# Graph attention on one core: edge features and gathered rows in one tile, one 128-column product in the aggregation

## The chip, the cores and the metric

The kernel runs on one core of a Trainium2 chip. The metric is the device time of one execution in microseconds; three executions of the kernel before took 5133.07, 5138.95 and 5140.92 us, so the median is 5138.95 us. A core has TensorE (PE in the profile, with its weight loads shown apart as PEld), VectorE (DVE), ScalarE (ACT), GpSimd (POOL) and SyncE (SP), each with an instruction stream of its own that it works off in order, and 16 DMA engines that several queues feed.

## What is computed

A graph attention layer with a residual and a layer norm, over 12,500 nodes with 64 features and 400,000 edges with 64 features. The edges come sorted by their destination node `dst`; `src` is random.

```python
h_src = nfeats[src]
h_dst = nfeats[dst]
z_att = jnp.concatenate([h_src, h_dst, efeats], axis=-1)
e = jax.nn.leaky_relu(z_att @ W_attn + b_attn, negative_slope=0.01)[:, 0]
m = jnp.concatenate([h_src, efeats], axis=-1) @ W_ne
emax = jax.ops.segment_max(e, dst, num_segments=N)
ex = jnp.exp(e - emax[dst])
denom = jax.ops.segment_sum(ex, dst, num_segments=N)
alpha = ex / denom[dst]
z = jax.ops.segment_sum(alpha[:, None] * m, dst, num_segments=N)
out = jax.nn.relu(jnp.concatenate([nfeats, z], axis=-1) @ W_out)
return _layernorm(nfeats + out)
```

The kernel sums `alpha * [efeats, h_src]` by destination first (128 numbers per node, in the on-chip tensor `acc`, nodes along its columns) and multiplies by `W_ne` and `W_out` at the end.

## The kernel before

**Tiling.** Edges are worked on in groups of 512 (`GE`): 128 partitions (`P`) with `T` = 4 edges each. There are 782 groups. `SG` = 4 groups make a part, and `BG` = 32 groups, eight parts, a chunk. The 26 chunks have 30, 23 times 32, 12 and 4 groups. Since the edges are sorted, the edges of a group belong to few neighbouring nodes: a window of `S` = 48 nodes that starts at the group's first destination.

**Gather (L134 to L150).** For each part SP starts one DMA (L140) that loads the edges' features into a tile `ze` of [128, 4 groups, 4, 64] floats; a partition's four edges lie side by side in memory, so a group gives each partition a piece of 1 KB. POOL then issues 16 indirect DMAs (L149), one for each group and `t`, that fetch for each partition one row of a table in memory (64 node features and the source's attention term, 65 floats) into a second tile `zx` of [128, 4, 4, 65]. In the first chunk, where `plain` is true, the table doesn't exist yet; the rows come from `x`, and the source term is computed by DVE. Both tiles come from the pool `feats` with 11 buffers each (`ZB`): the eight parts of a chunk and three parts ahead. The gathers of a part can start when the part 11 earlier has been aggregated. `indices` (L112 to L118) turns the `src` numbers into the index tile `srcs`, two chunks ahead.

**Scores (L155 to L184).** SP loads a small row of window values (`wrow`, L159), PE spreads it over the partitions (`win`, L161), and DVE multiplies the edge features by their attention weights and sums them (L165, L167), adds the source term, which is column 64 of `zx` (L172), makes the one-hot mask `hot` of each edge's node in its window (L174), and takes the destination's term through the mask (L179, L182).

**Softmax (L224 to L319).** It runs once per chunk, for all eight parts: maxima and sums along sorted edges by scans on DVE, with small PE products (L190, L198, L247) between them. It ends in `alpha`, one weight per edge, and a factor `fac` that rescales what the last chunk left in a node that goes on.

**Aggregate (L321 to L342).** For each part DVE multiplies `hot` by `alpha` into `w` (L324, two buffers). PE then does, for each of the 16 pairs of group and `t`, two products into one PSUM tile `pg` (two buffers): stationary `ze` (64 columns) into partitions 0 to 63 and stationary `zx` (64 of its 65 columns) into partitions 64 to 127, each with the 48 columns of `w` moving, accumulated over `t` (L332). In float32 each is done in two passes, so it shows as two weight loads and two products. DVE adds each group's 48 columns to `acc` at the window's place (L342).

**Order.** `main` (L460 to L487) walks over the chunks: for each part of the chunk its tiles and scores, then the indices of the chunk two ahead, the softmax, and the aggregations. The order on each engine comes from a scheduler at build time, so on DVE and PE the aggregations of a chunk stand between the scores of the next one. From the third chunk on, 25 aggregations are each followed by `own_part`, which computes a piece of the nodes' own part of the result (L441 to L450). After the last chunk `finish_sorted` multiplies `acc` by the weights (L538) and does the norm.

Of the kernel before, what the change touches and what calls it, by code (L numbers as in the profile page):

```python
# [27 lines left out]
SG = 4  # L28
HQ = 4
EW = 65  # L30
ZB = 11
HB = 9
NBC = 4
# [5 lines left out]
def sorted_path(ctx, tc, x, dst, idx, edge, w_ne, w_attn, b_attn, w_out, out, flag):  # L39
# [6 lines left out]
    nc = tc.nc  # L46
    N, D = x.shape
# [6 lines left out]
    RP = REST // T  # L54
# [24 lines left out]

    table = dram.tile([NB * P, EW], F32, name="table")  # L80
    early = dram.tile([NB * P, D], F32, name="early")
# [51 lines left out]

    def gather(g0, n, srcs, b0, plain):  # L134

        ze = feats.tile([P, SG, T, D], F32, name="ze")
        zx = feats.tile([P, SG, T, EW], F32, name="zx")
        whole = min(n, NG - 1 - g0)
        if whole:
            nc.sync.dma_start(out=ze[:, 0:whole].rearrange("p g t f -> p g (t f)"),  # L140
                              in_=edge[g0 * GE:(g0 + whole) * GE, :].rearrange("(g p t) f -> p g (t f)", g=whole, t=T))
        if whole < n:
            nc.vector.memset(ze[:, n - 1], 0.0)
            nc.sync.dma_start(out=ze[0:RP, n - 1],
                              in_=edge[E - REST:E, :].rearrange("(p t) f -> p t f", t=T))
        for g in range(n):
            for t in range(T):
                at = srcs[:, t, g0 + g - b0:g0 + g - b0 + 1]
                nc.gpsimd.indirect_dma_start(  # L149
                    out=zx[:, g, t, 0:D] if plain else zx[:, g, t, :], out_offset=None,  # L150
                    in_=x[:, :] if plain else table[:, :],
                    in_offset=bass.IndirectOffsetOnAxis(ap=at, axis=0))
        return ze, zx

    def scores(g0, n, ze, zx, drel, b0, y, plain):  # L155

        b = g0 - b0
        wrow = tiny.tile([1, SG, S], F32, name="wrow")
        nc.sync.dma_start(out=wrow[:, 0:n, :], in_=wins[g0:g0 + n, :].unsqueeze(0))  # L159
        win = psum.tile([P, SG, S], F32, name="win", bufs=1)  # L160
        nc.tensor.matmul(win[:, 0:n, :], ones_row, wrow[:, 0:n, :], start=True, stop=True)  # L161

        yb = y[:, :, b:b + n].rearrange("p t g -> p g t")
        prod = work.tile([P, SG, T, D], F32, name="prod", bufs=1)
        nc.vector.tensor_tensor(prod[:, 0:n], ze[:, 0:n],  # L165
                                w_edge.unsqueeze(1).to_broadcast([P, n, T, D]), op=OP.mult)
        nc.vector.tensor_reduce(yb, prod[:, 0:n], axis=AX.X, op=OP.add)  # L167
        if plain:
            nc.vector.tensor_tensor(prod[:, 0:n], zx[:, 0:n, :, 0:D],
                                    w_src.unsqueeze(1).to_broadcast([P, n, T, D]), op=OP.mult)  # L170
            nc.vector.tensor_reduce(zx[:, 0:n, :, D], prod[:, 0:n], axis=AX.X, op=OP.add)
# [12 lines left out]
        nc.vector.scalar_tensor_tensor(yb, sdst[:, 0:n], SLOPE, sdst[:, 0:n], op0=OP.mult, op1=OP.max)  # L184
        return hot
# [135 lines left out]
    def aggregate(g0, n, ze, zx, hot, alpha, b0, fac):  # L321
        b = g0 - b0
        w = work.tile([P, SG, T, S], F32, name="w")
        nc.vector.tensor_tensor(  # L324
            w[:, 0:n], hot[:, 0:n],
            alpha[:, :, b:b + n].rearrange("p t g -> p g t").unsqueeze(3).to_broadcast([P, n, T, S]),
            op=OP.mult)
        pg = psum.tile([P, SG, P], F32, name="pg")[:, :, 0:S]
        for g in range(n):
            for t in range(T):  # L330
                for at, z in ((0, ze), (D, zx)):
                    nc.tensor.matmul(pg[at:at + D, g, :], z[:, g, t, 0:D], w[:, g, t, :],  # L332
                                     start=(t == 0), stop=(t == T - 1))
# [16 lines left out]
    while left > 0:  # L350
# [12 lines left out]
                        in_=dst[(NW - 1) * P * GE:E].rearrange("(e o) -> e o", o=1)[0:E - (NW - 1) * P * GE:GE, :])  # L363
# [13 lines left out]
    with tc.tile_pool(name="pre", bufs=2) as pre:  # L377
        d0f = pre.tile([1, NG], F32, name="d0f", bufs=1)
        nc.vector.tensor_copy(d0f, d0i)
        for g0 in range(0, NG, 3 * P):  # L380
            n = min(3 * P, NG - g0)
# [3 lines left out]
        for c0 in range(0, NB, CB):  # L385
            c1 = min(c0 + CB, NB)
            f1 = min(c1, NFULL)
            n = c1 - c0
            xt = pre.tile([P, CB, EW], F32, name="xt", bufs=3)
            if c1 > NFULL:  # L390
                nc.vector.memset(xt[:, NFULL - c0:NB - c0, :], 0.0)
                nc.scalar.dma_start(out=xt[0:TAIL, NFULL - c0, 0:D], in_=x[NFULL * P:N, :])
            if f1 > c0:
                nc.scalar.dma_start(
                    out=xt[:, 0:f1 - c0, 0:D],
                    in_=x[c0 * P:f1 * P, :].rearrange("(b p) f -> p b f", p=P))
            for k, to in ((0, xt[:, 0:n, D]), (1, sd[:, c0:c1])):
                prod = pre.tile([P, CB, D], F32, name="prod")
# [5 lines left out]
                out=table[c0 * P:c1 * P, :].rearrange("(b p) f -> p b f", p=P),  # L404
                in_=xt[:, 0:n, :])
# [9 lines left out]
        while len(ahead) < 5 and (len(ahead) + 1) * SG <= sizes[0]:  # L415
            ahead.append(gather(len(ahead) * SG, SG, prepared[0][0], 0, True))
        over = sdflat[0:1]
        nc.sync.dma_start(out=shifted, in_=bass.AP(over.tensor, over.offset, [[1, NB * P], [1, S]]))
        for k in range(NW):
# [3 lines left out]
                out=wk, out_offset=None, in_=shifted[:, :],  # L423
# [32 lines left out]
    def prepare(k):  # L456
        srcs, pp = prepared.pop(k) if k in prepared else indices(starts[k], sizes[k])
        return srcs, slots_of(starts[k], sizes[k], pp)

    with loop:  # L460
        carry = None
        own = 0
        ready = {k: prepare(k) for k in range(2)}
        for k, G in enumerate(sizes):
            b0 = starts[k]
            srcs, drel = ready.pop(k)
            d3 = neighbours(b0, G)
            y = rows.tile([P, T, BG], F32, name="y", bufs=2)
            if G < BG:
                nc.vector.memset(y[:, :, G:BG], 0.0)  # L470
            parts = []
            for g0 in range(b0, b0 + G, SG):
                n = min(SG, b0 + G - g0)
                ze, zx = ahead.pop(0) if ahead else gather(g0, n, srcs, b0, k == 0)
                hot = scores(g0, n, ze, zx, drel, b0, y, k == 0)
                parts.append((g0, n, ze, zx, hot))
# [3 lines left out]
            for g0, n, ze, zx, hot in parts:  # L480
                aggregate(g0, n, ze, zx, hot, alpha, b0, fac if g0 == b0 else None)
# [524 lines left out]
```

## Time and profile before

The profiled execution took 5109.14 us; its span, from the first instruction to the last, is 5107.4 us. TensorE's granted clock was 0.547 of full speed as a mean, and 0.5 in most slices. PEclk in the profile is that clock.

| What | Value |
|---|---|
| median of the runs | 5138.95 us |
| profiled execution | 5109.14 us |
| its span | 5107.4 us |
| PE busy with products / loads, 14,238 of each | 1410.6 / 1105.0 us |
| of these the aggregation's (L332), 12,512 of each | 1595.7 / 1410.3 us by single instructions, which overlap |
| POOL busy, 3,142 instructions | 2964.9 us |
| DVE busy, 4,006 instructions | 1708.1 us |
| gathers from the table (L149) | 3,008, 944 ns each |
| DMA queue of POOL (q0) | 100,320 packets, 104.41 MB, 10.6% |
| DMA queue of SP (q1) | 147,464 packets, 116.22 MB, 8.0% |
| DMA queue of ACT (q10) | 67,280 packets, 16.45 MB, 1.6% |
| edge loads (`ze`) | 194 of 512 KB, three smaller ones |

Queue shares are the time of the packets as a share of 16 engines' time over the span. In the answers about single instructions a line gives start and duration in microseconds, engine, line and operation, the tiles written and read, and, in brackets, how long the engine was idle before and what ended that. "issue" is time in which the engine waited for nothing that the profile shows, and "remote" is a semaphore whose sender the profile can't tell. The table of stretches gives, for each stretch, its length, the busy time of each engine with the number of instructions that started, the clock, the share of the DMA engines and their GB/s.

### The profile page before, as it was taken

What the parts mean: (1) busy time and instruction counts of PE and PEld (TensorE: products, weight loads), DVE (VectorE), ACT (ScalarE), POOL (GpSimd) and SP (SyncE); (2) the same over time, 40 slices, a digit from 0 to 9 for tenths busy, and PEclk for the clock granted to TensorE, in tenths of its full rate; (3) what the DMA queues carried; (4) which work ended last, traced back from release to release, by engine and by line L of the source; (5) the groups of instructions that cost most, each with busy time, mean ns of one, the idle gap of its engine ahead of it and who ended that gap; (6) DMA issues with size and microseconds to landing.
All of it is one profiled execution on the core that took longest, in us unless ns stands there. A gap on an engine that the chain in (4) does not pass through costs nothing.

```text
span 5107.4 us, 39846 instructions
## 1 busy us (share of the span) xinstructions
PE 1410.6 (28%) x14238; PEld 1105.0 (22%) x14238; DVE 1708.1 (33%) x4006; ACT 109.6 (2%) x239; POOL 2964.9 (58%) x3142
## 2 busy tenths in 40 slices
PE   0022233443222222222222222222222222222226
PEld 0012122332222122212121212122222211221225
DVE  3333233232342332332323323323233233233346
ACT  0000000000000000000000000000000000000001
POOL 6645656556556556565565565655655655656550
PEclk9975555555555555555555555555555555555555
DMA  6111122222111112111111111111111211212113
GB/s 145 25 34 42 44 48 54 53 53 60 41 45 44 43 38 48 42 46 41 43 44 43 42 44 43 43 42 44 47 41 40 47 42 38 47 37 48 41 36 77
DMA packets 315273, 239.73 MB, mean 47 GB/s; under 512 B 160576, under 2 KB 264235, under 8 KB 315064
## 3 DMA queue, kind: packets, MB, share of 16 engines
q0 software_dynamic: 100320, 104.41, 10.6%
q1 hardware_dynamic: 147464, 116.22, 8.0%
q10 hardware_dynamic: 67280, 16.45, 1.6%
q8 instruction: 115, 1.88, 0.2%
q14 instruction: 94, 0.77, 0.1%
HBM read 226.98 MB, written 12.28 MB: 47 GB/s over the span
## 4 chain that ended last, share of the span: by engine, by line
issue 28%; POOL 26%; another core or an unknown queue 19%; DVE 14%; PE 10%; DMA 3%; DVEq 1%; ACT 0%; POOLq 0%; ACTq 0%
POOL zx L149 26%; PE pg L332 7%; DMA zx<-table,srcs 2%; DVE y L167 2%; DVE prod L165 2%; DVE sdst L182 1%; DVE prod L179 1%; PE sm L198 1%; PE sm L190 1%; DVE hot L174 1%; DVE w L324 1%; DVE by_row L195 0%; DVE b L271 0%; DVE acc L342 0%
## 5 line engine op out<-in xcount | busy, mean ns | idle before, releaser
L149 POOL DMA_INDIRECT zx<-table,srcs x3008 | 2840.6, 944 | 1951.4 <-issue 841.3
L332 PE MATMUL pg<-w,ze 128*64 128x48 f32 x6256 | 792.3, 297 | 1640.2 <-issue 985.1
L332 PEld LDWEIGHTS pg<-w,ze 128*64 128x64 f32 x6256 | 703.6, 213 | 1729.3 <-issue 1581.7
L332 PE MATMUL pg<-w,zx 128*64 128x48 f32 x6256 | 803.4, 297 | 613.2 <-issue 582.1
L324 DVE TENSOR_TENSOR w<-hot,alpha 128x768 f32<-128x768 bf16 x196 | 184.0, 949 | 2208.2 <-remote 1135.9
L332 PEld LDWEIGHTS pg<-w,zx 128*64 128x64 f32 x6256 | 706.7, 213 | 656.3 <-issue 621.7
L342 DVE TENSOR_TENSOR acc<-acc,pg 128x48 f32 x782 | 153.9, 197 | 812.7 <-remote 742.1
L161 PE MATMUL win<-wrow,ones_row 1*128 1x192 f32 (+1 forms) x392 | 182.0, 552 | 746.8 <-DVE prod L179 433.1
L161 PEld LDWEIGHTS win<-wrow,ones_row 1*128 1x128 f32 x392 | 92.9, 284 | 810.4 <-DVE prod L179 448.3
L165 DVE TENSOR_TENSOR prod<-ze,fixed 128x1024 f32<-128x1024 f32 x196 | 236.9, 1209 | 19.9 <-issue 19.9
L167 DVE TENSOR_REDUCE y<-prod 128x16 f32<-128x1024 f32 x196 | 236.1, 1205 | 2.4 <-DVE y L184 2.3
L182 DVE TENSOR_REDUCE sdst<-prod 128x16 f32<-128x768 f32 x196 | 185.1, 944 | 4.3 <-DVE prod L179 2.4
L179 DVE TENSOR_TENSOR prod<-hot,win 128x768 f32<-128x768 bf16 x196 | 185.4, 946 | 0.9 <-issue 0.2
L174 DVE TENSOR_TENSOR hot<-fixed,drel 128x768 bf16<-128x768 f32 x196 | 185.6, 947 | 0.0
L149 POOL DMA_INDIRECT zx<-in_x_dram,srcs x120 | 116.9, 974 | 51.5 <-issue 36.3
L112 ACT ACTIVATE nat<-raw 32x1024 f32<-32x1024 int32 (+3 forms) x26 | 27.5, 1056 | 3242.2 <-PE pp L115 1762.9
L450 PE MATMUL pg<-wout,xtt 64*128 64x64 f32 x196 | 47.4, 418 | 132.0 <-ACT xtt L447 132.0
L198 PE MATMUL sm<-ones_row,by_row 1*128 1x1 f32 x208 | 59.2, 351 | 81.2 <-DVE by_row L195 66.2
L198 PEld LDWEIGHTS sm<-ones_row,by_row 1*128 1x128 f32 x208 | 50.9, 302 | 131.5 <-DVE by_row L195 104.2
L190 PE MATMUL sm<-order,b 128*1 128x128 f32 x104 | 30.1, 391 | 163.8 <-DVE b L271 158.4
L450 PEld LDWEIGHTS pg<-wout,xtt 64*128 64x128 f32 x196 | 42.8, 319 | 148.3 <-ACT xtt L447 148.3
L190 PE MATMUL sm<-order,s 128*1 128x128 f32 x104 | 30.3, 393 | 147.7 <-issue 57.1
(133 smaller groups left out, 949.1 us busy)
## 6 DMA issues: line engine op xcount, KB each, us to landing
ze<-in_edge_dram SPq DMA_DIRECT2D x194, 512.0 KB
zx<-table,srcs POOLq DMA_INDIRECT x3008
table<-xt ACTq DMA_DIRECT2D x14, 227.5 KB
wrow<-wins SPq DMA_DIRECT2D x195, 0.8 KB
xb<-in_x_dram ACTq DMA_DIRECT2D x24, 128.0 KB
early<-xo ACTq DMA_DIRECT2D x24, 128.0 KB
xb<-in_x_dram ACTq DMA_DIRECT2D x12, 256.0 KB
xo<-early SPq DMA_DIRECT2D x12, 256.0 KB
```

The costliest lines, as they stand in the source:

```text
L149: nc.gpsimd.indirect_dma_start(out=zx[:, g, t, 0:D] if plain else zx[:, g, t, :], out_offset=None, in_=x[:, :] if plain else table[:, :], ...
L161: nc.tensor.matmul(win[:, 0:n, :], ones_row, wrow[:, 0:n, :], start=True, stop=True)
L165: nc.vector.tensor_tensor(prod[:, 0:n], ze[:, 0:n], w_edge.unsqueeze(1).to_broadcast([P, n, T, D]), op=OP.mult)
L167: nc.vector.tensor_reduce(yb, prod[:, 0:n], axis=AX.X, op=OP.add)
L174: nc.vector.tensor_tensor(hot[:, 0:n], slots.unsqueeze(1).unsqueeze(1).to_broadcast([P, n, T, S]), drel[:, :, b:b + n].rearrange("p t g -> ...
L179: nc.vector.tensor_tensor(at[:, 0:n], hot[:, 0:n], win[:, 0:n].unsqueeze(2).to_broadcast([P, n, T, S]), op=OP.mult)
L182: nc.vector.tensor_reduce(sdst[:, 0:n], at[:, 0:n], axis=AX.X, op=OP.add)
L190: nc.tensor.matmul(p[0:1, :], col, order, start=True, stop=True)
L198: nc.tensor.matmul(p[:, 0:1], by_row, ones_row[:, 0:1], start=True, stop=True)
L324: nc.vector.tensor_tensor(w[:, 0:n], hot[:, 0:n], alpha[:, :, b:b + n].rearrange("p t g -> p g t").unsqueeze(3).to_broadcast([P, n, T, S]) ...
L332: nc.tensor.matmul(pg[at:at + D, g, :], z[:, g, t, 0:D], w[:, g, t, :], start=(t == 0), stop=(t == T - 1))
L342: nc.vector.tensor_tensor(ag, ag, pg[:, g, :], op=OP.add)
```

## The change

The two tiles become one, `z`, of [128, 4, 4, 129] floats (`ZW` = 129), from the same pool with 11 buffers: columns 0 to 63 hold the edge's features, 64 to 127 the gathered node's, and column 128 its attention term. It takes as many bytes as the two did.

- The edge load becomes one DMA per group, 4 per part, of 128 KB each. A partition's four edges still lie side by side in memory (1 KB), but in the tile they stand 516 bytes apart, in pieces of 256 bytes.
- The gathers write into columns 64 to 128 of `z`; their number and size stay.
- The scores read the same numbers out of `z`, at its stride.
- The aggregation does one product per group and `t`, with the 128 columns of `z` as the stationary operand, into all 128 partitions of `pg`, where it did two with 64 columns each.

```diff
+ZW = 129
...
-        ze = feats.tile([P, SG, T, D], F32, name="ze")
-        zx = feats.tile([P, SG, T, EW], F32, name="zx")
+        z = feats.tile([P, SG, T, ZW], F32, name="z")
         whole = min(n, NG - 1 - g0)
-        if whole:
-            nc.sync.dma_start(out=ze[:, 0:whole].rearrange("p g t f -> p g (t f)"),
-                              in_=edge[g0 * GE:(g0 + whole) * GE, :].rearrange("(g p t) f -> p g (t f)", g=whole, t=T))
+        for g in range(whole):
+            nc.sync.dma_start(out=z[:, g, :, 0:D],
+                              in_=edge[(g0 + g) * GE:(g0 + g + 1) * GE, :].rearrange("(p t) f -> p t f", t=T))
...
                 nc.gpsimd.indirect_dma_start(
-                    out=zx[:, g, t, 0:D] if plain else zx[:, g, t, :], out_offset=None,
+                    out=z[:, g, t, D:2 * D] if plain else z[:, g, t, D:ZW], out_offset=None,
...
-        nc.vector.tensor_tensor(prod[:, 0:n], ze[:, 0:n],
+        nc.vector.tensor_tensor(prod[:, 0:n], z[:, 0:n, :, 0:D],
                                 w_edge.unsqueeze(1).to_broadcast([P, n, T, D]), op=OP.mult)
...
-        nc.vector.tensor_tensor(yb, yb, zx[:, 0:n, :, D], op=OP.add)
+        nc.vector.tensor_tensor(yb, yb, z[:, 0:n, :, 2 * D], op=OP.add)
...
         for g in range(n):
             for t in range(T):
-                for at, z in ((0, ze), (D, zx)):
-                    nc.tensor.matmul(pg[at:at + D, g, :], z[:, g, t, 0:D], w[:, g, t, :],
-                                     start=(t == 0), stop=(t == T - 1))
+                nc.tensor.matmul(pg[:, g, :], z[:, g, t, 0:2 * D], w[:, g, t, :],
+                                 start=(t == 0), stop=(t == T - 1))
```

More of the change, by code (lines that the diff above doesn't have):

```diff
@@ L134, in gather @@
     def gather(g0, n, srcs, b0, plain):
-        ze = feats.tile([P, SG, T, D], F32, name="ze")
-        zx = feats.tile([P, SG, T, EW], F32, name="zx")
+        z = feats.tile([P, SG, T, ZW], F32, name="z")
         whole = min(n, NG - 1 - g0)
-        if whole:
-            nc.sync.dma_start(out=ze[:, 0:whole].rearrange("p g t f -> p g (t f)"),
-                              in_=edge[g0 * GE:(g0 + whole) * GE, :].rearrange("(g p t) f -> p g (t f)", g=whole, t=T))
+        for g in range(whole):
+            nc.sync.dma_start(out=z[:, g, :, 0:D],
+                              in_=edge[(g0 + g) * GE:(g0 + g + 1) * GE, :].rearrange("(p t) f -> p t f", t=T))
         if whole < n:
-            nc.vector.memset(ze[:, n - 1], 0.0)
-            nc.sync.dma_start(out=ze[0:RP, n - 1],
+            nc.vector.memset(z[:, n - 1, :, 0:D], 0.0)
+            nc.sync.dma_start(out=z[0:RP, n - 1, :, 0:D],
                               in_=edge[E - REST:E, :].rearrange("(p t) f -> p t f", t=T))
@@ L149, in gather, with scores @@
                 nc.gpsimd.indirect_dma_start(
-                    out=zx[:, g, t, 0:D] if plain else zx[:, g, t, :], out_offset=None,
+                    out=z[:, g, t, D:2 * D] if plain else z[:, g, t, D:ZW], out_offset=None,
                     in_=x[:, :] if plain else table[:, :],
                     in_offset=bass.IndirectOffsetOnAxis(ap=at, axis=0))
-        return ze, zx
-    def scores(g0, n, ze, zx, drel, b0, y, plain):
+        return z
+    def scores(g0, n, z, drel, b0, y, plain):
         b = g0 - b0
@@ L168, in scores @@
         if plain:
-            nc.vector.tensor_tensor(prod[:, 0:n], zx[:, 0:n, :, 0:D],
+            nc.vector.tensor_tensor(prod[:, 0:n], z[:, 0:n, :, D:2 * D],
                                     w_src.unsqueeze(1).to_broadcast([P, n, T, D]), op=OP.mult)
-            nc.vector.tensor_reduce(zx[:, 0:n, :, D], prod[:, 0:n], axis=AX.X, op=OP.add)
-        nc.vector.tensor_tensor(yb, yb, zx[:, 0:n, :, D], op=OP.add)
+            nc.vector.tensor_reduce(z[:, 0:n, :, 2 * D], prod[:, 0:n], axis=AX.X, op=OP.add)
+        nc.vector.tensor_tensor(yb, yb, z[:, 0:n, :, 2 * D], op=OP.add)
         hot = work.tile([P, SG, T, S], BF16, name="hot", bufs=HB)
@@ L319, in softmax, with aggregate @@
         return alpha, fac, (top[:, R:R + 1], den[:, R:R + 1])
-    def aggregate(g0, n, ze, zx, hot, alpha, b0, fac):
+    def aggregate(g0, n, z, hot, alpha, b0, fac):
         b = g0 - b0
@@ L473, in sorted_path @@
                 n = min(SG, b0 + G - g0)
-                ze, zx = ahead.pop(0) if ahead else gather(g0, n, srcs, b0, k == 0)
-                hot = scores(g0, n, ze, zx, drel, b0, y, k == 0)
-                parts.append((g0, n, ze, zx, hot))
+                z = ahead.pop(0) if ahead else gather(g0, n, srcs, b0, k == 0)
+                hot = scores(g0, n, z, drel, b0, y, k == 0)
+                parts.append((g0, n, z, hot))
             if k + 2 < len(sizes):
@@ L479, in sorted_path @@
             alpha, fac, carry = softmax(G, y, d3, carry, k == 0)
-            for g0, n, ze, zx, hot in parts:
-                aggregate(g0, n, ze, zx, hot, alpha, b0, fac if g0 == b0 else None)
+            for g0, n, z, hot in parts:
+                aggregate(g0, n, z, hot, alpha, b0, fac if g0 == b0 else None)
                 if own < NB and k > 1:
```

## The prediction

> **What bounds the kernel now.** I read the page's busy shares first, then the chain of waits, then the gathers' line with what its idle time ended on, then one chunk of the middle along POOL and PE.
>
> ```profile
> PE 1410.6 (28%) x14238; PEld 1105.0 (22%) x14238; DVE 1708.1 (33%) x4006; ACT 109.6 (2%) x239; POOL 2964.9 (58%) x3142
> ...
> issue 28%; POOL 26%; another core or an unknown queue 19%; DVE 14%; PE 10%; DMA 3%; DVEq 1%; ACT 0%; POOLq 0%; ACTq 0%
> ```
>
> No engine is full; POOL is nearest. It only issues gathers, on a fixed beat:
>
> ```profile
> L149 POOL DMA_INDIRECT zx<-table,srcs x3008: 938/944/1131, 175.2 to 4969.6; - x188
> ...
>   PE pg L332: 786.6, 62
>   remote: 252.8, 80
> ```
>
> ```profile
> 2204.00 0.95 POOL L149 DMA_INDIRECT zx<-table,srcs  x1 [0.30 <-issue]
> 2211.60 0.94 POOL L149 DMA_INDIRECT zx<-table,srcs  x1 [6.64 <-PE pg L332]
> 2212.85 0.94 POOL L149 DMA_INDIRECT zx<-table,srcs  x1 [0.30 <-issue]
> ...
> 2320.82 0.94 POOL L149 DMA_INDIRECT zx<-table,srcs  x1 [20.97 <-PE pg L332]
> ```
>
> The beat is 0.944 + 0.30 = 1.247 us, so a part (16 gathers) takes 19.97 us, a chunk of eight parts 160, and all 3,128 gathers 3,901. The rest of the profiled 5,109 is about 150 us before the first and after the last gather, and 786.6 + 252.8 less 142 usual pauses of 0.30, 997 us, in which POOL waits for a slot that an aggregation by PE has to release. In the chunk shown (first gathers at 2118.7 and 2320.8, 202 us apart) the waits above 0.30 are 6.7, 6.3, 2.6, 3.0 and 2.9 us between aggregations, 21.5 together, and 20.7 while DVE finishes the softmax. The full chunks repeat this within about a microsecond.
>
> Why is PE, 28% busy, late? The table of stretches for the aggregation's line alone, for part 0 (no gathers in flight), a stretch with gathers, and the wait after it:
>
> ```profile
> core 0: us, PE busy (x) PEld busy (x), PEclk, DMA share, GB/s
> 2114.70:2118.50 3.80, 3.75 (x70) 3.75 (x72) 0.50 0.07 14
> ...
> 2138.40:2158.40 20.00, 1.91 (x8) 1.45 (x8) 0.50 0.14 27
> 2158.40:2165.30 6.90, 2.28 (x25) 1.89 (x24) 0.50 0.02 5
> ```
>
> The clock is 0.50 in all three, yet 70 products start in 3.8 us without gathers and 8 in 20 us with them. The timeline of PE shows the change of pace:
>
> ```profile
> 2136.71 0.31 PE L332 MATMUL pg<-w,ze 128*64 128x48 f32 x1
> 2139.19 0.24 PE L332 MATMUL pg<-w,zx 128*64 128x48 f32 x1 [2.17 <-issue]
> 2141.99 0.24 PE L332 MATMUL pg<-w,ze 128*64 128x48 f32 x1 [2.56 <-issue]
> ```
>
> Starts of loads and products in that stretch fall on a grid of 0.70 us (2137.80, 2139.19, 2140.59, 2141.99, 2142.70), about one record per one or two steps, until 4 us after the last gather was issued. What makes the grid the trace does not say.
>
> **The change, part by part.**
>
> *Half the PE instructions.* A part had 16 x 2 logical products of two passes, each a load and a product: 128 instructions; it will have 64. Part 2 of this chunk ran about 62 instructions at full pace from 2135.08, then some 26 to 38 grid steps to 2163.69, then the last 40 at full pace. If a step costs 0.70 us per instruction whatever its width, 64 instructions are the 62 fast ones and at most a few steps: done near 2143 instead of 2165. The lower bound is that nothing is saved: a load of 128 columns takes two steps where one of 64 took one, and 64 x 2 is again 128 steps. The rows lie nearer the first: the load (64 columns) and the product (48 rows) hold the same grid though they differ in size. I take the 21.5 us per chunk as gone, over 22 full chunks: -473 us; ends 0 and -542 (997 less 22 x 20.7).
>
> *One wide product for two narrow ones.* At full pace the two narrow tiles run side by side: part 0 of the next chunk starts at 2316.85 and is released at 2320.56, 3.7 us. The nearest row for a 128-column stationary is the final stage:
>
> ```profile
> 5039.63 17.33 PE L538 MATMUL po<-both,acc 128*128 128x64 f32 x80 [0.32 <-DVE both L520]
> ```
>
> 17.33 / 80 is 0.217 us per load and product with 64 moving rows; the load's share is about half (loads start 0.107 after a product), so 48 rows give 0.107 + 0.75 x 0.11 = 0.19, and 32 pairs 6.1 us: 2.4 us longer than today, with ends 0 (32 x 0.107 = 3.4, if load and product overlap) and +3.2 (0.217). It counts where POOL waits with no gathers in flight, at part 0 of each chunk after the first: 25 x 2.4 = +60 us (0 to +80). For the other parts it hides behind the 20 us of gathers; with that cover gone it is 2.4 us at each of 195 parts, +468.
>
> The Trainium skill speaks against this step: "TensorEngine Tiling (Array Packing)", sections Key Properties and Theoretical Speedup, says that different tiles load and multiply in parallel and that a dimension of 64 or less may gain up to 2x. By it undoing the split doubles 3.7 us to 7.4 and the +60 becomes 93. The trace agrees on the narrow side (ze and zx products start 0.01 us apart); the wide side no row of this kernel shows at 48.
>
> *Edge loads.* One DMA of 512 KB in 1-KB pieces becomes four of 128 KB in 256-B pieces. SP issues one in 0.37 to 0.39 us (2132.87), so 3 x 0.38 = 1.1 us more per part, ahead of the window row's load and the next loads in SP's queue; SP waits most of the time for releases, so 0 on the path. On the queues:
>
> ```profile
> q1 hardware_dynamic: 147464, 116.22, 8.0%
> q10 hardware_dynamic: 67280, 16.45, 1.6%
> ```
>
> Engine time per packet is 8.0% x 16 x 5107 / 147,464 = 44 ns on q1 and 19 ns on q10, whose packets are mostly 245 B. A part's edges take 512 x 44 / 16 = 1.4 us now and 2,048 x 19 / 16 = 2.4 us then, up to 5.6 at 44 ns: +1.0 to +4.2 us of transfer. It starts with the part's first gather and has the 20 us of the other gathers as cover, since the scores need both: 0. POOL kept its beat at 2133.68 while the edge load that SP issued at 2132.87 ran. Without that cover: +195 to +820.
>
> The skill's "DMA: Bandwidth & Descriptors", Why small descriptors are slow (HBM only), gives 27% overhead for 256-byte descriptors; by it alone 1.4 us would become 1.8. The rows above allow for more, and they decide.
>
> *Waits and DVE.* The new tile holds the 129 columns of the two old ones; gathers, sums and DVE's operations stay, and a wider stride changes no element count: 0. The first gather of a part gets waits on the old edge loads of its slot, which landed some 200 us before. A semaphore event on POOL takes 0.043 us and at 2223.995 it lay inside the 0.30 us pause: 0, at most 354 more of them x 0.043 = +15. SP's in-order queue sees the same release as today.
>
> **Sum.** 5109 - 473 + 60 = 4,696 in the profiled execution; the median of the runs is 5138.95 / 5109.14 = 1.0058 of it, so 4,723, say **4,720**. The softmax's wait of 20.7 us stays: after the last release DVE still has some 41 us of scores and softmax (2279.8 to 2320.5), of which a part of gathers covers 20.
>
> **Rivals.**
>
> *Slower: the grid stays and the wide product comes on top.* If steps go by columns, every release still waits for the gathers to stop, and then the burst that ends the part is serial. Price 2.4 us at the six of eight releases that POOL waits for, 146 in all, +351: 5,460, runs 5,490; at all 195 parts +468, runs 5,610. It decides if a 128-column load takes 1.4 us on the grid. For it: part 5's records end at 2218.7 and yet its release comes at 2233.9, 2.6 us after the last gather's issue, as if the end of the flow and not the count set it; chunks with additional PE work keep gaps of 3.4 us. Against: part 1 was released at 2132.9 in the midst of the flow.
>
> *The count does not matter and nothing else bites.* The gaps stay, part 0 pays 2.4: 5,169, runs 5,200, 1.2% slower; with overlap of load and product no change.
>
> *All waits go.* With releases early, DVE reaches the last scores as soon as they land, 100 us into a chunk of 160, and 41 us later the softmax is done: no wait at all. 5109 - 22 x 42.2 = 4,181, runs 4,205. Against: at 28 grid steps per 20 us of gathers PE can't do 64 instructions a part without some pause.
>
> **Chances.** Forecast 0.34 (its own range 4,480 to 4,930), all waits gone 0.16, count without effect 0.14, slower 0.36. Leaving out the outer ends of both: 4,250 to 5,550. A difference of about 0.2% is what a measurement here can tell from none. Faster 0.50 (the first two), same 0.04 (from the count without effect, with overlap), slower 0.46.
>
> **What would show it.** Right: POOL's idle time on PE's aggregation falls from 1,039 towards 550 us, a wait of some 23 us per chunk remains, q1 has about 450,000 packets, and aggregations end in mid-flow. Wrong: loads 1.4 us apart on the grid, or five gaps per chunk as before and each longer; gathers off their 1.247 beat while q1 runs; part 0 at 3.7 us or above 7.

## The result, and the profile after

The changed kernel took 5315.73 us (median of 4 runs, 5298.48 to 5325.86), the kernel before in the same comparison 5137.34 us: a ratio of 1.034, 95% interval 1.032 to 1.037. It is slower by 3.4%, where 4,720 us, 8% faster, was forecast. The profiled execution has a span of 5296.8 us, 189.4 us more than that of before.

The experiments showed that chips differ here. On some the kernel before takes 5,121 to 5,137 us, as in the first comparison; on others 4,104 to 4,111 us. The difference lies in how PE fares while gathers are in flight. I call them the slow and the quick kind; every ratio below is taken on one chip. The experiments ran on eight chips, four of each kind, each on one occasion only; that the chip itself makes the difference is likely but not shown. On the quick kind the variants with the wide product lose 1.1%; the changed kernel itself was not run there.

The page of the changed kernel, its busy shares, chain, gathers, products and two queues:

```profile
PE 1879.7 (35%) x7982; PEld 1675.6 (32%) x7982; DVE 1719.2 (32%) x4006; ACT 107.9 (2%) x239; POOL 2961.6 (56%) x3142
...
q0 software_dynamic: 100320, 104.41, 12.9%
q1 hardware_dynamic: 456824, 116.26, 10.2%
...
another core or an unknown queue 44%; issue 15%; POOL 13%; DVE 12%; PE 10%; DMA 2%; ACTq 2%; DVEq 1%; ACT 0%; POOLq 0%; SPq 0%
...
L331 PE MATMUL pg<-w,z 128*128 128x48 f32 x6256 | 1381.7, 409 | 1795.7 <-DVE acc L341 1072.5
```

The change does what it says: PE has 7,982 products where it had 14,238, and q1 moves the same bytes in 456,824 packets. But PE's busy time goes up, from 1410.6 to 1879.7 us: two narrow products ran side by side, and a wide one runs alone. What POOL waited for, from the gathers' line:

```profile
L149 POOL DMA_INDIRECT z<-table,srcs x3008: 938/944/1087, 174.9 to 5121.6; - x188
...
  PE pg L331: 861.2, 45
  remote: 295.0, 57
```

102 waits instead of 142, but 1,156 us instead of 1,039. The beat of the gathers has stayed at 944 ns. One chunk of the middle on POOL:

```profile
2122.88 0.94 POOL L149 DMA_INDIRECT z<-table,srcs  x1 [6.26 <-PE pg L331]
...
2161.57 0.95 POOL L149 DMA_INDIRECT z<-table,srcs  x1 [0.30 <-issue]
2194.12 0.95 POOL L149 DMA_INDIRECT z<-table,srcs  x1 [31.60 <-PE pg L331]
```

The pauses between aggregations now come once in two parts, about 6 us each, instead of five per chunk; that is where fewer instructions helped. The wait for the softmax has grown from 21 to 31 us. I summed all POOL waits above the usual 0.30 us from the starts of the gathers in the two traces (per chunk: means of chunks 7 to 23, which have no work of `own_part`):

| us | before | after | difference |
|---|---|---|---|
| waits for the softmax, all (per chunk) | 538.9 (20.9) | 751.6 (30.5) | +212.7 |
| waits between aggregations, all (per chunk) | 496.7 (21.7) | 443.5 (17.9) | -53.2 |
| from the last gather to the last aggregation | 64.9 | 101.3 | +36.4 |
| from there to the end | 72.0 | 73.0 | +1.0 |

The rows make +196.9, where the span grew by 189.4. The first gather starts 1.9 us earlier, the gathers' own time is 3.3 us less in all, and about 2 us are left over in small pauses.

### The profile page after: what moved, and what is told of

Its sections match the earlier page's. It is cut to its first block, busy times and chain, and to the rows that moved or that the text cites. A ratio compares the mean times of both kernels' runs of the same rounds, so it can differ in the third digit from the quotient of the medians.

```text
span 5296.8 us, 29642 instructions
## 1 busy us (share of the span) xinstructions
PE 1879.7 (35%) x7982; PEld 1675.6 (32%) x7982; DVE 1719.2 (32%) x4006; ACT 107.9 (2%) x239; POOL 2961.6 (56%) x3142
## 3 DMA queue, kind: packets, MB, share of 16 engines
q1 hardware_dynamic: 456824, 116.26, 10.2%
## 4 chain that ended last, share of the span: by engine, by line
another core or an unknown queue 44%; issue 15%; POOL 13%; DVE 12%; PE 10%; DMA 2%; ACTq 2%; DVEq 1%; ACT 0%; POOLq 0%; SPq 0%
POOL z L149 13%; PE pg L331 7%; DVE prod L165 2%; ACTq L113 1%; DVE y L167 1%; DVE sdst L182 1%; DMA z<-table,srcs 1%; PE sm L198 1%; PE sm L190 1%; DVE prod L179 1%; DVE hot L174 1%; PE win L161 1%; DVE acc L341 0%; DVE by_row L195 0%
## 5 line engine op out<-in xcount | busy, mean ns | idle before, releaser
L149 POOL DMA_INDIRECT z<-table,srcs x3008 | 2838.1, 944 | 2108.5 <-PE pg L331 861.2
L331 PE MATMUL pg<-w,z 128*128 128x48 f32 x6256 | 1381.7, 409 | 1795.7 <-DVE acc L341 1072.5
L331 PEld LDWEIGHTS pg<-w,z 128*128 128x128 f32 x6256 | 1361.1, 330 | 1869.7 <-DVE acc L341 1080.3
L161 PE MATMUL win<-wrow,ones_row 1*128 1x192 f32 (+1 forms) x392 | 196.0, 593 | 536.0 <-issue 379.7
L165 DVE TENSOR_TENSOR prod<-z,fixed 128x1024 f32<-128x1024 f32 x196 | 238.5, 1217 | 16.4 <-issue 16.0
L190 PE MATMUL sm<-order,s 128*1 128x128 f32 x104 | 30.5, 396 | 441.0 <-issue 310.4
L149 POOL DMA_INDIRECT z<-in_x_dram,srcs x120 | 116.1, 968 | 49.6 <-issue 36.0
L256 DVE TENSOR_TENSOR_SCAN s<-pf,e 128x128 f32<-128x128 f32 x26 | 11.0, 423 | 291.2 <-ACT e L254 235.3
L190 PE MATMUL sm<-order,b 128*1 128x128 f32 x104 | 30.5, 395 | 130.7 <-DVE b L271 99.7
```

The costliest lines, as they stand in the source:

```text
L149: nc.gpsimd.indirect_dma_start(out=z[:, g, t, D:2 * D] if plain else z[:, g, t, D:ZW], out_offset=None, in_=x[:, :] if plain else table[:, :],
L165: nc.vector.tensor_tensor(prod[:, 0:n], z[:, 0:n, :, 0:D], w_edge.unsqueeze(1).to_broadcast([P, n, T, D]), op=OP.mult)
L190: nc.tensor.matmul(p[0:1, :], col, order, start=True, stop=True)
L331: nc.tensor.matmul(pg[:, g, :], z[:, g, t, 0:2 * D], w[:, g, t, :], start=(t == 0), stop=(t == T - 1))
```

## Where the three differences come from

**The wide product itself.** The table of stretches for the aggregation's line, for part 0 after the softmax and for the time behind the last gather of the changed kernel, then for the latter in the one before. The columns are the stretch, its length, busy time and number of products, of loads, the clock, the share of the DMA engines and GB/s. The 1.00 of the first two lines is no measurement (see the last section):

```profile
2186.70:2194.10 7.40, 7.32 (x35) 7.32 (x35) 1.00 0.04 7
5122.50:5223.80 101.30, 62.67 (x288) 61.71 (x288) 1.00 0.01 1
```

```profile
4970.60:5035.40 64.80, 26.96 (x606) 25.85 (x607) 0.66 0.02 3
```

Part 0 starts at 2186.78 and POOL goes on at 2194.12, 7.3 us later, where it was 4.0 (2316.85 to 2320.82): 3.4 us at each chunk's softmax, over 80 us in all. Behind the last gather nine more parts (288 products of 32 a part) follow one after the other; PE is busy 62.7 us there instead of 27.0, and this +35.7 is the +36.4 of the table. The pace can be read off any of them:

```profile
5128.41 7.06 PE L331 MATMUL pg<-w,z 128*128 128x48 f32 x32 [10.81 <-DVE acc L341]
```

7.06 / 32 is 0.22 us per load and product, as in the final stage with 64 moving rows (0.217): the 16 rows less save nothing. Part of the +35.7 can be the clock's and not the width's: in that stretch of the kernel before it was 0.66 as a mean, and its pairs of narrow products start 0.107 us apart at 0.50 and 0.058 at 1.00, while the wide products at full pace are 0.21 us apart throughout. At 0.50 the 303 pairs would have taken 32 us instead of 27, an estimate from these numbers.

**The waits between aggregations.** Two of the five waits per chunk are gone, the others have changed. In the kernel before, 34 of the 85 waits over 0.5 us in chunks 7 to 23 end 0.3 us after the recorded end of the last product of the part that POOL waits for; they are the long ones, 6.4 us each (23 of 101 in a second trace). The other 51 are for parts recorded done 2 to 20 us before. In the changed kernel all 52 waits are of this second sort: the part is recorded done 12 to 32 us before POOL goes on. PE's timeline before the wait that ends at 2122.88, and DVE's first use of the sum:

```profile
2092.34 7.06 PE L331 MATMUL pg<-w,z 128*128 128x48 f32 x32 [5.40 <-issue]
...
2104.74 0.24 PE L331 MATMUL pg<-w,z 128*128 128x48 f32 x1 [2.32 <-issue]
2107.55 0.24 PE L331 MATMUL pg<-w,z 128*128 128x48 f32 x1 [2.57 <-issue]
...
2122.64 0.21 DVE L341 TENSOR_TENSOR acc<-acc,pg 128x48 f32 x1 [24.36 <-PE pg L331]
```

The 32 products of the part in question run at full pace with gathers in flight and are recorded done at 2099.40. The last gather of the flow ends at 2116.6, and only 6 us after that do DVE and POOL go on, 23 us after the part's end. The products of the next part stand on the steps of the kernel before: 1.40 us from a load (2103.34) to its product (2104.74), as with half the columns (1.39, 2137.80 to 2139.19). So a wide instruction costs no more steps than a narrow one, and half as many are done sooner; the release does not follow them. What holds it back the traces do not say.

**The softmax's wait.** Its other 6 us per chunk start at PE's eight transposes of the indices (L116), which stand ahead of the softmax's first product in PE's queue:

```profile
2141.70 1.01 PE L116 MATMUL pp<-ident,nat 32*128 32x32 f32 x8
...
2163.46 1.05 ACT L113 ACTIVATE nat<-raw 32x1024 f32<-32x1024 int32 x1 [186.48 <-remote]
2164.42 0.40 ACT L254 ACTIVATE e<-er 128x128 f32<-128x128 f32 x1
...
2164.85 0.42 DVE L256 TENSOR_TENSOR_SCAN s<-pf,e 128x128 f32<-128x128 f32 x1 [18.93 <-ACT e L254]
```

```profile
2289.89 1.00 PE L115 MATMUL pp<-ident,nat 32*128 32x32 f32 x8
...
2290.98 1.05 ACT L112 ACTIVATE nat<-raw 32x1024 f32<-32x1024 int32 x1 [177.27 <-PE pp L115]
```

In the second fence, the kernel before, ACT goes on 0.1 us after the last transpose. In the first, the changed kernel, the transposes are recorded done at 2142.7, and ACT's copy, which waits for their semaphore, starts at 2163.46, 0.9 us after POOL's last gather of the part. The exponential `e` stands behind that copy in ACT's queue and DVE's scan behind `e`: 18.93 us of idle DVE that before did not have. From the recorded end of the transposes to the copy it is 0.1 us as a median of the 21 later copies before (and in a second trace of the same kernel), and 18.9 us after (19.3 in a second trace).

What goes with it is how long gathers have been in flight when the transposes run. I put together eight traces of the slow kind in which they keep their place. Where they end about 11 us after a pause of the gathers, the copy follows within 0.9 us in 63 of 67 cases, in both kernels. Where they end 19 to 21 us after one, it follows 12 to 24 us later in all 74 cases, from 6.4 us before to 4.5 us after the end of that flow of gathers, also with the narrow products of m5_fewer. Before, a pause of 3 us lay right ahead of the part in which the transposes run; now, with pauses in pairs, that part follows its forerunner without one.

## The experiments

Each is a small edit of one of the two kernels. "Before" in the table is the kernel before on the same chip; waits are in us per full chunk, and the tail is the time from the last gather to the last aggregation.

| run | kind of chip | before | this | ratio (95%) | softmax | between | tail |
|---|---|---|---|---|---|---|---|
| c_after | slow | 5130.4 | 5312.67 | 1.036 (1.034 to 1.038) | 30.5 | 17.9 | 101.4 |
| c_before | slow | 5130.4 | 5132.02 | 1.000 (1.000 to 1.002) | 20.7 | 21.9 | 63.6 |
| g1_narrow | slow | 5129.9 | 5177.39 | 1.009 (1.007 to 1.011) | 22.3 | 22.8 | 67.5 |
| g3_nat2 | slow | 5129.9 | 5299.57 | 1.033 (1.031 to 1.034) | 30.1 | 18.4 | 101.3 |
| h8_later | slow | 5134.59 | 5233.92 | 1.020 (1.018 to 1.022) | 26.1 | 18.2 | 93.9 |
| h4_onewait | slow | 5134.59 | 5308.65 | 1.034 (1.032 to 1.035) | 31.1 | 17.3 | 103.5 |
| m5_fewer | slow | 5120.94 | 5112.50 | 0.999 (0.997 to 1.000) | 25.1 | 16.3 | 64.9 |
| e1_narrow | quick | 4104.4 | 4096.73 | 0.998 (0.997 to 0.999) | 0.0 | 0.0 | 46.4 |
| f1_narrow | quick | 4110.96 | 4102.82 | 0.998 (0.997 to 0.999) | 0.0 | 0.0 | 46.3 |
| e2b_pieces | quick | 4104.4 | 4096.52 | 0.998 (0.997 to 0.999) | 0.0 | 0.0 | 46.9 |
| e3_nat2 | quick | 4104.4 | 4148.48 | 1.011 (1.009 to 1.012) | 0.0 | 0.0 | 90.1 |
| f3_nat2 | quick | 4110.96 | 4154.85 | 1.011 (1.009 to 1.012) | 0.0 | 0.0 | 90.1 |
| e4a_onewait | quick | 4104.4 | 4151.30 | 1.011 (1.010 to 1.013) | 0.1 | 0.0 | 92.3 |
| f4_onewait | quick | 4110.96 | 4156.52 | 1.011 (1.010 to 1.013) | 0.1 | 0.0 | 92.1 |
| f5_fewer, k5_fewer | quick | 4110.96, 4105.26 | 4110.45, 4105.29 | 1.000 (0.999 to 1.001), both | 0.0 | 0.0 | 46.9, 46.3 |
| k8b_later, n8b_later | quick | 4105.26, 4105.7 | 4100.5, 4101.3 | 0.999 (0.998 to 1.000), both | 0.0 | 0.0 | 45.5, 45.4 |

**The two kernels again, with their traces.**

> The changed kernel itself, on the chip of the experiments. Theory A (the wide product costs 3.1 to 3.7 us wherever no gather covers it): as much above the kernel before as the two variants with the wide product, 1.1%, nearly all of it behind the last gather; where PE is slow in the flow of gathers as in the first comparison, 3.4%. Rival (the loss of 3.4% does not depend on PE's pace): 3.4% on this chip too.

> The kernel before itself, for its trace on the chip of the experiments. Where it takes about 4,104 us: POOL's beat without a wait in chunks 2 to 23, no steps of 0.70 us on PE, and aggregations released in mid-flow. Where it takes about 5,137 us: the waits of the first profile.

Both ran on a chip of the slow kind and came out as in the first comparison. That the loss depends on PE's pace follows only from the runs on the quick kind below.

**Undo the product: narrow products from the one tile.** The tile, its semaphores for the loads and the four loads of 256-byte pieces stay.

```diff
-                nc.tensor.matmul(pg[:, g, :], z[:, g, t, 0:2 * D], w[:, g, t, :],
-                                 start=(t == 0), stop=(t == T - 1))
+                for at in (0, D):
+                    nc.tensor.matmul(pg[at:at + D, g, :], z[:, g, t, at:at + D], w[:, g, t, :],
+                                     start=(t == 0), stop=(t == T - 1))
```

> The one tile and the four edge loads of 256-byte pieces stay; the aggregation does two 64-column products again. Theory A (the wide product makes the loss): about 5,140 to 5,170 us, part 0 released 3.7 us after it starts, the softmax's wait back at 21 us. Theory B (the edge loads make it): about 5,300 us, the wait still near 31 us.

> Again narrow products from the one tile with the four edge loads; the loads were shown to cost nothing on a chip where POOL never waits. Where PE is slow in the flow of gathers (the kernel before at about 5,130 us): theory A (wide product) about 5,130 to 5,160 us, rival B (edge loads) about 5,300 us.

> Narrow products from the one tile with the four edge loads. On a chip where the kernel before takes about 5,130 us: theory A (wide product) 5,130 to 5,160 us, rival B (edge loads) about 5,300 us. On a chip where it takes about 4,104: 4,096 us as twice measured.

On the slow kind 1.009 instead of 1.036: three quarters of the loss go when the wide product is undone (theory A), though 17 us more are left than A allowed. On the quick kind nothing is lost, 0.2% is won. So the wide product, its width and its halved count together, makes 2.7 points of 3.6, and what came with the tile, the loads with their pieces and waits, 0.9 where PE's completions are late (softmax 1.6 us and the other waits 0.9 us more per chunk than in c_before) and nothing elsewhere.

**Only the loads.** Two tiles and narrow products, four loads per part in 256-byte pieces.

```diff
-        ze = feats.tile([P, SG, T, D], F32, name="ze")
+        ze = feats.tile([P, SG, T, EW], F32, name="ze")
...
+        for g in range(whole):
+            nc.sync.dma_start(out=ze[:, g, :, 0:D],
+                              in_=edge[(g0 + g) * GE:(g0 + g + 1) * GE, :].rearrange("(p t) f -> p t f", t=T))
```

> Two tiles and narrow products as before, but the edge features come in four loads per part of 256-byte pieces (the tile of the edges is padded to 65 columns). Theory A (wide product): 5,137 us give or take 15, no change. Theory B (edge loads): about 5,300 us. If the loads cost only their transfer, 1 to 4 us at each part, 5,330 to 5,960.

This ran on the quick kind, where POOL hardly waits at all:

```profile
L149 POOL DMA_INDIRECT zx<-table,srcs x3008: 940/945/1094, 174.2 to 3976.7; - x188
...
  PE pg L332: 41.5, 2
```

Two waits on the aggregation instead of 62; the gathers end at 3977.7 us, 3,963 us after the first, close to the 3,901 of their beat. There the four loads cost nothing, and the narrow variant gives the same time. It was not run on the slow kind, so the 0.9% is not divided between the pieces and the tile.

**A second buffer for `nat`.** To make room, `own_part` goes by 3 blocks.

```diff
-        nat = chunks.tile([BG, P * 2 * T], F32, name="nat", bufs=1)
+        nat = chunks.tile([BG, P * 2 * T], F32, name="nat", bufs=2)
```

> The changed kernel with two buffers for the index tile nat (own_part's blocks go 3 at a time to make room, which touches chunks 2 to 6 only). Theory C (the softmax starts late since ScalarE's copy into nat waits for the semaphore of PE's eight transposes and the softmax's exponential stands behind it in ScalarE's queue): softmax's wait from 31 to about 24 us per chunk, 22 x 7 = 160 us less, about 5,155 us. Rival (the softmax would be as late from its own small products): about 5,300 us, the wait still near 31.

> Again the changed kernel with two buffers for nat. Where PE is slow in the flow: theory C (ScalarE's copy behind PE's transposes holds up the softmax) the softmax's wait from 31 to about 24 us, about 5,155 us; rival about 5,300 us. Elsewhere 4,148 us again.

> The changed kernel with two buffers for nat. On a chip where the kernel before takes about 5,130 us: theory C (ScalarE's copy behind PE's transposes holds up the softmax) the softmax's wait from 31 to about 24 us, about 5,155 us; rival about 5,300 us. Otherwise 4,148 us as twice measured.

A miss, for a reason in the edit: the scheduler put the copy one chunk further ahead, where it waits for the very same transposes. ACT's copy in g3_nat2 starts 23.4 us after the transposes' last record, as late as without the edit:

```profile
2171.39 1.06 ACT L113 ACTIVATE nat<-raw 32x1024 f32<-32x1024 int32 x1 [189.22 <-remote]
```

It tells nothing against the theory. On the quick kind it shows the price of the wide product alone: e3_nat2 takes 51.8 us more than e1_narrow, which has the same tile and loads, 43.7 of them in the tail (90.1 us for 46.4) and the other 8.1 in waits for the softmax (49.0 us for 40.9, all in the first chunks).

**Transposes out of the softmax's way.** The index copy is tied behind the weights `w` of the chunk's third part, so the transposes follow the first part's products.

```diff
+        if after is not None:
+            nc.vector.tensor_copy(nat[0:1, 0:1], after[0:1, 0, 0, 0:1])
         nc.scalar.activation(nat[0:G], raw[0:G], AF.Copy)
...
-            if k + 2 < len(sizes):
-                ready[k + 2] = prepare(k + 2)
...
+                if k + 2 < len(sizes) and g0 == b0 + 2 * SG:
+                    ready[k + 2] = prepare(k + 2, wt)
```

> The changed kernel with the index copy and its eight transposes tied behind the weights of the chunk's third part, so that PE does them after the first part's products and not before the softmax's. Where the kernel before takes about 5,130 us: theory C (the transposes' late semaphore holds up the softmax) the softmax's wait from 31 to about 24 us, 22 x 7 = 160 us less than 5,313, about 5,150 us, less what the transposes cost in their new place; rival about 5,310 us. Where it takes about 4,104: 4,150 us.

The softmax's wait falls by 4.4 us per chunk (30.5 to 26.1) and the time by 1.6 points. One such wait on POOL, which was 31.60 us in the changed kernel:

```profile
2168.43 0.95 POOL L151 DMA_INDIRECT z<-table,srcs  x1 [26.89 <-PE pg L333]
```

Theory C named the right place with too high a price: of the 9.6 us that the wait has grown, 4.4 go with the transposes, 3.4 are part 0's longer product, and some 1.8 are left, to which no run was put.

**One wait per part.** In the changed program 3,037 of the aggregation's 6,256 weight loads carry a wait, and 3,030 of its products update PE's own semaphore; with one small product ahead of them 262 and 210 are left.

```diff
+        nc.tensor.matmul(pgw[0:1, 0, S:S + n * T], w[:, 0, 0, 0:1], z[:, 0:n, :, 2 * D],
+                         start=True, stop=True)
```

> The changed kernel with one small extra product per part that reads a column of all 16 gathers first, so that the 16 wide products carry no wait on a gather's semaphore and no semaphore update of their own (98 times fewer of each). Theory D (PE is slow in the flow of gathers because each product waits on, or updates, a semaphore): five to six waits of POOL per chunk vanish or shrink, 4,700 to 5,000 us. Rival (the pace of PE in the flow has another cause): 5,316 us give or take 40.

> Again the changed kernel with one product per part that waits for all its gathers, the 16 wide products without waits and updates of their own. Where PE is slow in the flow: theory D (waits on gathers' semaphores or updates make the steps) 4,200 to 5,000 us; rival 5,310 us give or take 40. Elsewhere 4,151 us again.

> The changed kernel with one product per part that waits for all its gathers, the 16 wide products without waits and updates of their own. Where the kernel before takes about 5,130 us: theory D (waits on gathers' semaphores or updates make PE slow in the flow) 4,200 to 5,000 us; rival 5,310 us give or take 40. Where it takes about 4,104: 4,151 us as twice measured.

5308.65 us on the slow kind: theory D falls. Neither the waits nor the updates of single products make PE slow there.

**Fewer instructions, still narrow.** The kernel before with the second product only at t = 0, which leaves out three quarters of the gathered rows' sum: 80 instead of 128 instructions per part.

```diff
-                for at, z in ((0, ze), (D, zx)):
+                for at, z in ((0, ze), (D, zx))[0:2 if t == 0 else 1]:
                     nc.tensor.matmul(pg[at:at + D, g, :], z[:, g, t, 0:D], w[:, g, t, :],
-                                     start=(t == 0), stop=(t == T - 1))
+                                     start=(t == 0), stop=(at > 0 or t == T - 1))
```

> The kernel before with the gathered rows' product at t = 0 only, so three quarters of that half's sum are left out: 80 instead of 128 instructions of the aggregation per part, all narrow. Theory E (the number of PE's instructions in the flow sets the waits, as the prediction took it): where PE is slow, the waits between aggregations shrink by a third or more, 4,700 to 5,000 us. Rival (the end of the flow sets them): 5,130 us give or take 30. Elsewhere 4,104 us less up to 15.

> The kernel before with the gathered rows' product at t = 0 only, so three quarters of that half's sum are left out: 80 instead of 128 instructions of the aggregation per part, all narrow. Where the kernel before takes about 5,130 us: theory E (the number of PE's instructions in the flow sets the waits) the 21.7 us between aggregations shrink by a third or more and the softmax's wait with them, 4,700 to 5,000 us; rival (the pause of the gathers sets them) 5,130 us give or take 40. Where it takes about 4,104: 4,110 us as measured.

> Narrow products, 80 instead of 128 instructions of the aggregation per part (the gathered rows' product at t = 0 only, three quarters of that half's sum left out). Where the kernel before takes about 5,130 us: theory E (the number of PE's instructions in the flow sets the waits) 4,700 to 5,000 us; rival (the pause of the gathers sets them) 5,130 us give or take 40. Otherwise 4,105 to 4,110 us as twice measured.

Two runs were on the quick kind and told nothing; the third is the most telling of the study. With more than a third of the products gone and none of them wide, the time is the same. POOL and ACT in the middle of m5_fewer:

```profile
2093.26 0.95 POOL L149 DMA_INDIRECT zx<-table,srcs  x1 [5.76 <-remote]
...
2157.31 0.94 POOL L149 DMA_INDIRECT zx<-table,srcs  x1 [24.41 <-PE pg L332]
```

```profile
2113.08 1.01 PE L115 MATMUL pp<-ident,nat 32*128 32x32 f32 x8
...
2128.48 1.06 ACT L112 ACTIVATE nat<-raw 32x1024 f32<-32x1024 int32 x1 [175.64 <-remote]
```

The pattern of the changed kernel is there without its wide product: pauses once in two parts, and ACT's copy 14.4 us behind the transposes (15.8 as a median of the 21 later copies). Against c_before the waits between aggregations are 105 us less in all (395.8 against 500.9), and the softmax's are 110 us more (654.3 against 544.8). What fewer instructions win between the parts, the softmax gives back.

**Transposes moved in the kernel before.** The edit of h8_later on the kernel before.

> The kernel before with the index copy and its transposes behind the weights of the chunk's third part. Where the kernel before takes about 5,130 us: the transposes' semaphore came 3 us late on average there, so about 3 us per chunk, 5,070 us; rival (their new place costs as much) 5,130 us. Where it takes about 4,104: no change, within 10 us.

> The kernel before with the index copy and its transposes behind the weights of the chunk's third part. Where the kernel before takes about 5,130 us: the transposes' semaphore came 3 us late on average there, so about 3 us per chunk less, 5,070 us; rival (the new place adds as much between the aggregations) 5,130 us give or take 20. Otherwise 4,100 us as measured.

Both were on the quick kind: 0.1% faster than before, and so than the changed kernel's variants. Whether it wins on the slow kind was not seen. The 3 us of the expectation are not in the copies: in the kernel before ACT's copy follows the transposes within 0.1 us in 20 of 21 chunks. No version was shown to beat both kernels on both kinds.

## Why the prediction was wrong

- **Half the PE instructions, -473 us.** This is the step that failed. It took all five waits of a chunk for the time that PE needs on the steps of 0.70 us, so that half the instructions would free the aggregations from the gathers. Only two of the five were that, 6.4 us each, and they are gone. The other three were for parts whose products were already recorded done, and such waits have grown: 12 to 32 us from a part's end to its release. In all, the waits between aggregations fell by 53 us only, and in m5_fewer, with 80 narrow instructions, by 105. In the lines above such a release comes only after the flow of gathers has ended, and two parts now share one pause. That a step costs the same whatever the width was right. The rival's argument, in the text itself, was right too: part 5's release 2.6 us after the last gather's issue, and the equal gaps in chunks with more PE work, spoke for the end of the flow.
- **"The softmax's wait of 20.7 us stays."** It did not: +212.7 us in all. The sum treated the aggregations and the softmax as separate, though the pause ahead of a chunk's last part was what let PE's transposes ahead of the softmax through in time. m5_fewer and h8_later show 4.4 us per chunk of that each, by bringing it about and by undoing it; DVE's last stretch before the softmax's end, 41 us then, got longer by its wait on ACT.
- **The wide product, +60 us.** Right in kind, too small in size and in place. Per part 7.06 us and 3.4 more than before, against 6.1 and 2.4 worked out; the bound of +3.2 was nearly the value, since fewer moving rows saved nothing. It counted at the softmax (over 80 us) and also at the nine parts behind the last gather (+36, some 5 of them the clock's), which the sum left out. The cover there is gone by the kernel's own end, and the text had priced "cover gone" without asking where that is.
- **Edge loads, 0.** Transfer after the change was sized well: 18.9 ns a packet, 2,048 x 18.9 / 16 = 2.4 us a part, as worked out. Before the change it was sized too low: the 44 ns are a mean over packets of several sizes, and the 1-KB packets alone took 54.8 ns, 1.75 us a part and not 1.4. On the quick kind 0 is right; on the slow kind loads and tile together cost 47 us (g1_narrow), between the 0 with cover and the +195 without. The rule of the Trainium skill in "DMA: Bandwidth & Descriptors" (Why small descriptors are slow (HBM only)), 27% overhead at 256 bytes, falls somewhat short here: four 256-byte packets take 74.6 ns where one of 1 KB takes 54.8, 36% more by these means, and 57% by the medians (18 and 46 ns).
- **Extra waits on POOL, 0.** Held: the beat stayed at 944 ns with a pause of 0.30.
- **The rivals.** The one on the slower side had the right half, releases bound to the gathers' pauses with the serial burst on top, at 5,490 us too dear: it charged 2.4 us at six releases a chunk, and the runs show it at the softmax and in the tail only. Its condition, that a wide load takes more steps than a narrow one, does not hold: 1.40 us from load to product in both. The Trainium skill's "TensorEngine Tiling (Array Packing)" (Key Properties, Theoretical Speedup), weighed there against the change, was borne out: without the split a part's products took 7.06 us for 3.7, close to the 2x, the 3.7 at a recorded clock of 0.50.

## What to carry to other kernels

Before pricing fewer instructions on an engine that others wait for, compare the end of its last instruction with the release, wait by wait. If releases come long after that end, and coincide with another queue falling idle, the count is not the price, and a saved pause can move the wait to the next stage. Two half-width products that run side by side in different columns were as cheap here as one of them (at the clock of 0.50, 0.107 us for a pair, and for a lone one in m5_fewer); merging them nearly doubled the time, and it shows first where nothing covers it, at a phase's first part and behind the last load. A copy that waits for another engine should not stand ahead of a critical operation in its queue, and a second buffer does not cure that if the scheduler spends it on running further ahead.

## What the runs showed of the hardware

- The same program takes 4,104 us on one chip and 5,130 on another. Gathers are equal on both (0.945 us to issue, 87 ns a packet for the kernel before and the narrow variant); what differs is PE. In the same kernel its idle time ahead of the aggregation's products that nothing in the profile explains ("issue") is 36.4 us in 20 pieces on the quick kind (e1_narrow) and 1113.0 us in 1,380 on the slow kind (g1_narrow). On the slow kind, transposes that end 19 to 21 us into a flow of gathers are reported 12 to 24 us late, in narrow and wide kernels alike; on the quick kind, where the flow hardly ever pauses, the copy follows the transposes within 0.1 us in all 21 chunks (e1_narrow). What sets the 0.70-us steps and the late reports, and why only some chips show them, stays open; the semaphore waits and updates of single products are ruled out as their cause (h4_onewait).
- In the kernel before, the recorded clock tells the pace of the narrow pairs: 0.107 us apart at 0.50, 0.058 at 1.00 (from 2119.59 us on). In the traces of the kernels with wide products no change of the clock is recorded at all, and the page has no row of it; the 1.00 that the tables show for them is not a measurement. Their pace speaks against it: the final stage's 80 products take 17.33 us in the changed kernel as in the kernel before, where 0.50 is recorded for them.
